# A scheduling edge that keeps the splits of a layer's q and k weights behind the exponentials written before them

## The chip, the cores and the metric

The kernel runs on one core of one Trainium2 chip. The metric is the device time of one launch in microseconds (us), taken as the median of several runs.

## The reference, cut to what matters

The program computes `x + attention(LN(x)) + stack(LN(x))` for 8 sequences of 512 tokens with 128 features. The attention has 16 heads of 8 features, relative positions and a causal mask. The stack has 6 layers, and nearly all of the time is spent in it. Each layer is a local attention (16 heads of 64 features, windows of 32 queries looking at 64 keys) and a gated feed-forward block:

```python
for i in range(DEPTH):                                   # DEPTH = 6
    x = attn_layer(shift_tokens(x), Wqkv[i], q_scale[i], k_scale[i], Wo[i]) + x
    x = ffn_layer(shift_tokens(x), ln_g[i], ln_b[i], W1[i], b1[i], W2[i], b2[i]) + x
# attn_layer: q, k, v = split(x @ Wqkv); q, k = l2norm(.) * scale, rotated by position
#   sim = q k^T * 8 in windows, masked; softmax; times v; @ Wo
# ffn_layer: layernorm, h = xn @ W1 + b1, a * gelu(gate) @ W2 + b2
```

Everything is float32, and the result must be that of float32.

## The kernel before

**Splits.** TensorE multiplies in a rounded form of float32 (the type F32R in the code). Where this is too coarse, an operand x is kept as two parts: hi, x rounded to that form, and lo = x - hi. A product is then three matmuls (`product`, lines 670 to 672). The function `split` makes the two parts: ScalarE copies x into hi (line 658), and another engine, VectorE if none is named, subtracts (line 659). For the projections of q and k, both the stream of x (`xs_hi`, `xs_lo`) and the weights (`wqk_hi`, `wqk_lo`) are split.

**Tiles.** The stack works through 192 tiles of 128 tokens: 6 layers, in each 8 sequences, in each 4 tiles. This text numbers the tiles of a layer 0 to 31, so tile 5 of layer 2 is its sixth. A tile has these steps: `project` (three matmuls into `qk_ps`; VectorE multiplies by the tables, lines 799 and 800, giving `q` and `rot`; ScalarE squares, line 801; GpSimd adds, lines 806 and 808), `normalise` (VectorE computes 1/norm in a chain of small steps, lines 821 and 75 to 86, the last of which gives `rn`; GpSimd multiplies q and k by it, line 826), `turn_q` and `turn_k` (transposes on TensorE, line 845; ScalarE copies, line 848), `scores` twice (masks by matmul, line 867; scores, line 879; VectorE takes maxima `mx`, line 888; ScalarE 8 exponentials `pr` with their sums, line 892; after the second time VectorE inverts the sums, line 904, GpSimd scales `pr`, line 905, and VectorE transposes it, line 907), `values` (line 921; the rows are then moved to `vw` by DMAs that SyncE's queue issues, line 923), `attend` and `add`. The feed-forward block of a finished sequence is laid between the steps of the next tiles, in pieces.

**Order.** TensorE's order is written out by hand: the strings `ORDERS` give the steps of a tile, with a period of four tiles, and the loop stands under `tc.manual_schedule(engines={nc.tensor.engine})`. On the other engines and in SyncE's DMA queue the order is chosen when the program is built: a planner runs through a timeline of its own and places an instruction where it finds it ready, which may be long before its place in the source. Each engine then runs its instructions strictly in that order, and waits in it. An edge added by `tc.add_manual_dep` with the class NoSync costs no semaphore; it only tells the planner that one instruction may not be placed before another.

Such edges exist already: `in_turn` chains the exponentials and the Gelus of the stack with each other, so that ScalarE's function tables are not exchanged more than needed. `last["any"]` holds the newest of them.

**The weights of the next layer.** While layer l is worked on, the weights of layer l+1 are fetched. The table `AHEAD` gives the place in the source:

```python
AHEAD |= {28 - 3 * c: ("projection", (c,)) for c in range(4)}
...
if n > -1 and left in AHEAD and l + 1 < DEPTH:
    step, args = AHEAD[left]
    fetch_of[step](l + 1, *args)
```

`left` is the number of tiles left in the layer. So in the source the four quarters c0 to c3 of `Wqk` are loaded and split at the start of the tiles 4, 7, 10 and 13 of the layer before. `load_projection` moves a quarter by DMA into a buffer `wqk_raw` and splits it. These buffers carry the tag `raw`, of which there are two in all; the two halves of W1 of the feed-forward block (`load`, tile 5 in the source, DMA line 680), the four quarters, and the blocks `wv_raw` and `wo_raw` (DMA lines 737 and 739) share them. A DMA into a `raw` buffer waits in SyncE's queue until the buffer's last user is done, for a quarter its subtraction, and the moves to `vw` issued later stand behind it. The parts hi and lo themselves have places of their own that alternate by layer. The quarters of layer 0 are loaded before any exponential of the stack.

Of the kernel before, what the change touches and what calls it, by code (L numbers as in the profile page):

```python
# [624 lines left out]
def steps_of_layers(ctx, tc, i, ident, ident_b, xt, out, spare):  # L625
    nc = tc.nc
# [8 lines left out]
    last = {}  # L635
# [17 lines left out]
            )  # L653
        last["any"] = ins

    def split(hi, lo, x, lo_engine=None):

        nc.scalar.copy(hi, x)
        (lo_engine or nc.vector).tensor_sub(lo, x, hi.bitcast(F32))  # L659

    def root_tile(n):
# [12 lines left out]
    def load(l):  # L674

        w = {}
        w["1"] = [p2.tile([P, 2 * DFF], F32R, name=f"w1_{k}", bufs=1) for k in ("hi", "lo")]
        for c in range(0, 2 * DFF, DFF):
            raw = wp.tile([P, DFF], F32, name="w1", tag="raw", bufs=2)
            nc.sync.dma_start(out=raw, in_=i["W1"][l, :, c : c + DFF])  # L680
            split(*(x[:, c : c + DFF] for x in w["1"]), raw)
        if VAR["D"]:
            raw = wp.tile([P, len(FCH), E], F32, name="w2", tag="raw", bufs=2)
        else:
            raw = w["2f"] = p2.tile([P, len(FCH), E], F32, name="w2", bufs=1)
        if VAR["D"]: w["2"] = [p2.tile([P, len(FCH), E], F32R, name=f"w2_{k}", bufs=1) for k in ("hi", "lo")]
        for n, (c, m) in enumerate(FCH):
            nc.sync.dma_start(out=raw[:m, n, :], in_=i["W2"][l, c : c + m, :])
        for n, (c, m) in enumerate(FCH if VAR["D"] else ()):
            split(*(x[:m, n] for x in w["2"]), raw[:m, n])  # L690

        w["g"] = p2.tile([P, 3], F32, name="wg")
        for n, k in enumerate(("ln_g", "ln_b", "b2")):
            nc.sync.dma_start(out=w["g"][:, n : n + 1], in_=i[k][l].unsqueeze(1))
        w["b1"] = p2.tile([P, 2, len(FCH)], F32, name="wb1")
        for a in range(2):
            for n, (c, m) in enumerate(FCH):
                nc.sync.dma_start(
                    out=w["b1"][:m, a, n : n + 1],
                    in_=i["b1"][l, a * DFF + c : a * DFF + c + m].unsqueeze(1),  # L700
                )
        return w
# [19 lines left out]
    def load_projection(l, c):  # L722

        raw = wp.tile([P, 512], F32, name="wqk_raw", tag="raw", bufs=2)
        nc.sync.dma_start(out=raw, in_=i["Wqk"][l, c])
        hi = by_turns[l % 2].tile([P, 512], F32R, name=f"wqk_hi{c}")
        lo = by_turns[l % 2].tile([P, 512], F32R, name=f"wqk_lo{c}")
        split(hi, lo, raw)
        projections.setdefault((l, c // 2), []).append((hi, lo))

    def load_values(l):
# [369 lines left out]
    for c in range(4):  # L1101
        load_projection(0, c)
        if c % 2:
            yield
# [40 lines left out]
    with tc.manual_schedule(engines={nc.tensor.engine}):  # L1145
        for n in range(-1, len(tiles) + 2):
# [11 lines left out]
            if n > -1 and left in AHEAD and l + 1 < DEPTH:  # L1158
                step, args = AHEAD[left]
# [127 lines left out]
```

## Time and profile before

| what | value |
|---|---|
| median of 3 runs | 3420.91 us (3416.99 to 3425.21) |
| profiled execution | 3422.36 us, of it 3420.6 us in the profile's span |
| granted TensorE clock, mean | 0.992 |
| TensorE matmul / VectorE / ScalarE / GpSimd busy | 94% / 88% / 81% / 80% of the span |
| one layer of the stack, tile 0 to tile 0 | 478 to 488 us |

In the profile PE is TensorE, PEld its weight loads, DVE VectorE, ACT ScalarE, POOL GpSimd and SP SyncE; L and a number is a line of the kernel. The profile is of one execution; its own time is 1.45 us over the median of the runs. Idle time is put down to the event that ended it, by semaphores. The busy time of TensorE is modelled from pipelined starts. Times of day such as 1509.59 are microseconds from the span's start.

### The profile page before, as it was taken

Reading aid. Unit: us, or ns where it says so; the run is one execution under the profiler, and the core shown is the slowest. Engines: PE = TensorE matmul, PEld = TensorE weight load, DVE = VectorE, ACT = ScalarE, POOL = GpSimd, SP = SyncE. Lnnn points to the kernel's source line nnn. Section 1 sums busy time; section 2 is a strip of 40 time slices with the busy share of each in tenths; the row PEclk is TensorE's granted clock in tenths of the full one; section 3 lists DMA queues with packets and bytes.
Section 4 is the critical chain, followed back from the end, with each engine's and each line's share of the span. In section 5 each row is a group of like instructions: output and inputs, shape, how many; then the busy total and the mean of one; then the engine's idle time right before and its main releaser. Section 6 shows DMA issues by size and latency. Waiting matters only on the chain.

```text
span 3420.6 us, 132912 instructions
## 1 busy us (share of the span) xinstructions
PE 3207.7 (94%) x51264; PEld 2394.4 (70%) x51264; DVE 2998.4 (88%) x7542; ACT 2783.2 (81%) x9786; POOL 2752.1 (80%) x2102
## 2 busy tenths in 40 slices
PE   7999979999999999999999999999999999999997
PEld 4667657777777777667777767777767777776775
DVE  7777788999999999899898998989999898998994
ACT  5777768888888888888888888888888888887884
POOL 6767668888888888788888888888888887887883
PEclk9999999999999999999999999999999999999998
DMA  2111123332333323333233332323333233332332
GB/s 59 37 40 46 48 72 74 75 73 72 89 82 78 74 71 79 84 87 75 69 75 78 83 87 69 77 70 86 82 80 76 69 78 77 81 80 75 83 75 58
DMA packets 221067, 250.07 MB, mean 73 GB/s; under 512 B 73238, under 2 KB 115604, under 8 KB 220436
## 3 DMA queue, kind: packets, MB, share of 16 engines
q1 hardware_dynamic: 220148, 241.18, 28.4%
q8 instruction: 407, 6.67, 0.9%
q14 instruction: 224, 1.84, 0.2%
q10 hardware_dynamic: 288, 0.39, 0.1%
HBM read 26.92 MB, written 4.19 MB: 9 GB/s over the span
## 4 chain that ended last, share of the span: by engine, by line
PE 43%; DVE 27%; ACT 18%; issue 4%; DMA 3%; POOL 3%; SPq 2%; ACTq 0%; POOLq 0%; DVEq 0%
ACT pr L892 8%; PE y_ps L941 8%; PE qkT_ps L845 6%; PE sc_ps L879 4%; DVE q L799 4%; DVE rot L800 4%; PE f_ps L1054 3%; PE v_ps L670 2%; PE v_ps L671 2%; PE v_ps L672 2%; ACT sq L801 2%; DVE pT L907 2%; DVE mx L888 2%; PE qk_ps L670 2%; ACT L892 2%
## 5 line engine op out<-in xcount | busy, mean ns | idle before, releaser
L892 ACT ACTIVATE pr<-sc_ps,mx 128x64 f32<-128x64 f32 x3072 | 923.4, 348 | 96.9 <-DVE mx L888 92.6
L806 POOL TENSOR_TENSOR q<-q,rot 128x1024 f32<-128x1024 f32 x380 | 924.8, 2434 | 91.8 <-DVE rot L800 62.9
L826 POOL TENSOR_TENSOR q<-q,rn 128x1024 f32<-128x1024 f32 x380 | 717.4, 1909 | 4.1 <-DVE rn L86 3.8
L892 ACT ACTIVATION_READ_ACCUMULATOR pr<-sc_ps,mx 128x1 f32 x3072 | 719.5, 241 | 0.0
L801 ACT ACTIVATE sq<-qk_ps 128x512 f32<-128x512 f32 x768 | 469.7, 633 | 262.1 <-DVE rot L800 157.6
L905 POOL TENSOR_TENSOR pr<-pr,sm 128x1024 f32<-128x1024 f32 x192 | 365.7, 1905 | 337.9 <-DVE rn L86 188.7
L799 DVE TENSOR_TENSOR q<-qk_ps,wrot 128x512 f32<-128x512 f32 x768 | 523.1, 681 | 48.1 <-PE qk_ps L672 43.3
L800 DVE TENSOR_TENSOR rot<-qk_ps,wrot 128x512 f32<-128x512 f32 x768 | 520.6, 678 | 0.0
L921 ACT COPY v<-v_ps 128x512 f32<-128x512 f32 x768 | 469.7, 660 | 48.8 <-PE v_ps L672 21.9
L845 PE MATMUL qkT_ps<-ident,q 128*128 128x128 f32 x3072 | 480.0, 282 | 24.8 <-POOL q L826 15.0
L845 PEld LDWEIGHTS qkT_ps<-ident,q 128*128 128x128 f32 x3072 | 340.3, 141 | 148.4 <-POOL q L826 58.0
L879 PEld LDWEIGHTS sc_ps<-kT,qT 64*32 64x32 f32 x24576 | 272.8, 105 | 183.2 <-issue 182.4
L941 PE MATMUL y_ps<-vw,pT 128*32 128x128 f32 x11904 | 382.0, 275 | 2.8 <-DMA vw<-v 2.8
L941 PEld LDWEIGHTS y_ps<-vw,pT 128*32 128x32 f32 x11904 | 327.6, 110 | 57.5 <-issue 28.5
L670 PE MATMUL qk_ps<-wqk_hi,xs_hi 128*128 128x512 f32 x768 | 347.1, 452 | 5.9 <-ACT sq L801 2.5
L670 PE MATMUL v_ps<-wvo_hi,xs_hi 128*128 128x512 f32 x768 | 338.8, 441 | 7.3 <-ACT ys L952 6.2
L879 PE MATMUL sc_ps<-kT,qT 64*32 64x64 f32 x24576 | 335.5, 225 | 0.0
L672 PE MATMUL qk_ps<-wqk_hi,xs_lo 128*128 128x512 f32 x768 | 304.5, 396 | 0.9 <-POOL xs_lo L659 0.9
L672 PE MATMUL v_ps<-wvo_hi,xs_lo 128*128 128x512 f32 x768 | 304.1, 396 | 0.0
L671 PE MATMUL qk_ps<-wqk_lo,xs_hi 128*128 128x512 f32 x768 | 303.7, 395 | 0.0
L671 PE MATMUL v_ps<-wvo_lo,xs_hi 128*128 128x512 f32 x768 | 302.7, 394 | 0.0
L888 DVE TENSOR_REDUCE mx<-sc_ps 128x4 f32<-128x256 f32 x768 | 282.4, 407 | 10.7 <-PE sc_ps L879 9.0
(206 smaller groups left out, 7058.9 us busy)
## 6 DMA issues: line engine op xcount, KB each, us to landing
vw<-v SPq DMA_DIRECT2D x3072, 64.0 KB
a_qz<-a_qT SPq DMA_DIRECT2D x128, 64.0 KB
wqk_raw<-in_Wqk SPq DMA_DIRECT2D x24, 256.0 KB
wv_raw<-in_WvT SPq DMA_DIRECT2D x12, 256.0 KB
wo_raw<-in_Wo SPq DMA_DIRECT2D x12, 256.0 KB
wrot<-in_trig SPq DMA_DIRECT2D x24, 128.0 KB
a_x<-in_x SPq DMA_DIRECT2D x8, 256.0 KB
a_res<-in_x SPq DMA_DIRECT2D x8, 256.0 KB
```

Source lines behind the costliest of these rows:

```text
L670: nc.tensor.matmul(ps, lhsT=ah, rhs=bh, start=True, stop=False)
L671: nc.tensor.matmul(ps, lhsT=ah, rhs=bl, start=False, stop=False)
L672: nc.tensor.matmul(ps, lhsT=al, rhs=bh, start=False, stop=True)
L799: nc.vector.tensor_mul(q[:, :, a], ps, wide(cos[:, a, :]))
L800: nc.vector.tensor_mul(v[:, :, 1 - a], ps, wide(sin[:, 1 - a, :]))
L801: nc.scalar.activation(sq[:, a], ps, AF.Square)
L806: adds.tensor_add(q, q, v)
L826: scales_by.tensor_mul(q, q, r[:, m, :].unsqueeze(2).to_broadcast([P, H, D]))
L845: nc.tensor.transpose(tr[:, m, :], q[:, 2 * hp : 2 * hp + 2, :].rearrange("p h d -> p (h d)"), ident)
L879: nc.tensor.matmul(ps[32 * j : 32 * j + 32, w, :], lhsT=qT[r, 4 * g + j, W * w : W * w + W], rhs=kT[r, 4 * g + j, W * w : W * w + 2 * W], ...
L892: nc.scalar.activation(pr[:, p, g, w, :], ps[:, w, :], AF.Exp, bias=mx[:, p, g, w : w + 1], accum_out=sm[:, m : m + 1],),
L941: nc.tensor.matmul(y[W * w : W * w + W, :], lhsT=pT[:, p, g, w, half, :], rhs=v[:, p, g, :], start=(p, g, half) == (0, 0, 0 if keys[w] is ...
```

## The change

`split` takes another argument, `after`. Where it is given, an edge without a semaphore keeps the ScalarE copy behind that instruction in the planned order. Only `load_projection` gives it: the newest exponential or Gelu at that place of the source. For layer 0 there is none yet. The subtraction has no edge of its own, but it reads the copy. The computation is unchanged.

```diff
-    def split(hi, lo, x, lo_engine=None):
+    def split(hi, lo, x, lo_engine=None, after=None):
 
-        nc.scalar.copy(hi, x)
+        step = nc.scalar.copy(hi, x)
+        if after is not None:
+            tc.add_manual_dep(
+                step.ins,
+                after.name,
+                mybir.DependencyInfo(mybir.DependencyClass.NoSync, mybir.DependencyReason.DATA),
+                reason="in its turn",
+            )
         (lo_engine or nc.vector).tensor_sub(lo, x, hi.bitcast(F32))
...
         lo = by_turns[l % 2].tile([P, 512], F32R, name=f"wqk_lo{c}")
-        split(hi, lo, raw)
+        split(hi, lo, raw, after=last.get("any"))
```

## The prediction, on record before the changed kernel ran

> **What bounds the kernel now.** I read the busy table and the chain of the page first.
>
> ```profile
> PE 3207.7 (94%) x51264; PEld 2394.4 (70%) x51264; DVE 2998.4 (88%) x7542; ACT 2783.2 (81%) x9786; POOL 2752.1 (80%) x2102
> PE 43%; DVE 27%; ACT 18%; issue 4%; DMA 3%; POOL 3%; SPq 2%; ACTq 0%; POOLq 0%; DVEq 0%
> ```
>
> TensorE carries the time, but more than half of the chain lies on others: it stands in its fixed order whenever VectorE's maxima or ScalarE's exponentials are late. Next I took the start of each tile's first mask matmul (line 867) from TensorE's timeline. Without weight work, four tiles of types 0, 1, 2, 3 (number modulo 4) take 13.9, 16.3, 13.1 and 16.2 us. The view by stretches, cut at such starts, shows what fills them (columns: length, then busy time of TensorE, its loads, VectorE, ScalarE, GpSimd):
>
> ```profile
> 1493.20:1507.90 14.70, 13.03 (x241) 9.92 (x241) 12.42 (x24) 12.61 (x40) 9.58 (x6) 1.00 0.34 90
> 1507.90:1528.30 20.40, 16.71 (x241) 11.20 (x241) 19.25 (x42) 16.05 (x61) 14.97 (x9) 1.00 0.40 100
> ...
> 1541.40:1557.60 16.20, 15.67 (x253) 11.81 (x253) 15.85 (x35) 13.60 (x50) 14.61 (x8) 1.00 0.29 72
> 1557.60:1571.50 13.90, 12.97 (x242) 9.93 (x242) 11.52 (x28) 13.30 (x47) 9.86 (x7) 1.00 0.28 69
> 1587.70:1600.80 13.10, 13.00 (x246) 10.38 (x246) 12.42 (x41) 11.23 (x46) 12.01 (x8) 1.00 0.39 95
> ...
> 2964.20:2982.20 18.00, 16.24 (x241) 11.33 (x240) 15.31 (x38) 14.76 (x59) 14.86 (x9) 1.00 0.29 71
> ```
>
> These are tiles 4, 5, 7, 8 and 10 of layer 2, then tile 5 of layer 5, which splits W1 but no q and k weights. Tile 5 of layer 2 is a burst: VectorE is busy for 19.25 us. Tile 7 has VectorE full, tile 10 TensorE and nearly VectorE, tile 8 leaves VectorE 2.4 us.
>
> The third view is the timeline of VectorE and GpSimd. The first three lines are subtractions in layer 0, the others in layer 2:
>
> ```profile
> 469.75 0.68 DVE L659 TENSOR_TENSOR wqk_lo<-wqk_raw,wqk_hi 128x512 fp32r<-128x512 f32 x1
> 471.01 2.19 DVE L659 TENSOR_TENSOR wqk_lo<-wqk_raw,wqk_hi 128x512 fp32r<-128x512 f32 x1
> 478.15 1.18 DVE L659 TENSOR_TENSOR wqk_lo<-wqk_raw,wqk_hi 128x512 fp32r<-128x512 f32 x1
> 1509.59 2.34 DVE L659 TENSOR_TENSOR wqk_lo<-wqk_raw,wqk_hi 128x512 fp32r<-128x512 f32 x1
> 1514.95 1.53 DVE L659 TENSOR_TENSOR wqk_lo<-wqk_raw,wqk_hi 128x512 fp32r<-128x512 f32 x1
> ```
>
> ```profile
> 1509.48 1.90 POOL L905 TENSOR_TENSOR pr<-pr,sm 128x1024 f32<-128x1024 f32 x1 [6.70 <-DVE root_ps L84]
> 1512.18 3.76 POOL L826 TENSOR_TENSOR q<-q,rn 128x1024 f32<-128x1024 f32 x2 [0.79 <-DVE rn L86]
> ```
>
> Alone a subtraction takes 0.68 us. Beside a GpSimd instruction it ends 0.55 us after that one: 1509.48 + 1.90 = 1511.38 against 1509.59 + 2.34 = 1511.93, and 1515.94 against 1516.48.
>
> **What moves.** TensorE's order stays. In the planned orders of the two programs, per layer 1 to 4: c0's copy goes from the end of the layer before (1430.0, just ahead of layer 2) to tile 4; c1 to c3 go from the burst in tiles 4 and 5 to the starts of tiles 7, 10 and 13. In layer 0, c0 moves from just before the stack, c1 to c3 from tile 0. No instruction is added. Each copy stands behind the previous tile's exponentials, ahead of `ys`; each subtraction inside or just behind the 1/norm chain.
>
> **What it saves.** c0's old place was free: tile 31 takes 18.24 us before layer 2 as before layer 5, where no c0 is. For c1 to c3, tiles 4 to 8 take 78.52, 78.22, 77.85 and 77.89 us in layers 1 to 4, mean 78.12, against 75.39 in layer 5: 2.73 us a layer, 10.9 in all. The three subtractions there took 0.70 + 2.34 + 1.53 = 4.57 us, so 0.60 of VectorE's time reached TensorE. In layer 0 the three took 0.68 + 2.19 + 1.18 = 4.05; at 0.60 that is 2.4 (bounds 0 and 4.05). Together 13.3 us.
>
> **What it costs.** I follow each subtraction at its new place in layer 2. The GpSimd instruction that runs at that moment:
>
> ```profile
> 1490.18 1.91 POOL L905 TENSOR_TENSOR pr<-pr,sm 128x1024 f32<-128x1024 f32 x1 [1.58 <-DVE root_ps L82]
> ...
> 1539.90 1.04 POOL L1002 TENSOR_TENSOR dg<-ident,rstd_lo 128x512 fp32r<-128x512 f32 x1
> ...
> 1585.67 1.91 POOL L905 TENSOR_TENSOR pr<-pr,sm 128x1024 f32<-128x1024 f32 x1 [0.84 <-DVE rn_s L81]
> ```
>
> - *c0, tile 4*, before line 84, which began at 1490.39. It ends at 1492.09 + 0.55 = 1492.64. The first `rot`, now two steps behind line 84, ends near 1494.15 instead of 1492.24. ScalarE's square waits for that `rot`, and Gelu, the exchange of tables and the exponentials stand behind it. TensorE's next scores waited 0.91 us for those exponentials: 1.9 us late. The planner also lets GpSimd's `xs_lo` and one addition pass ahead of the scaling of q: the transposes of q could then be 2.5 us late.
> - *c1, tile 7*, before line 82 (1540.32): it ends at 1540.94 + 0.55 = 1541.49. 1.2 us; VectorE then runs without a gap up to the maxima.
> - *c2, tile 10*, before line 85 (1586.29): it ends at 1588.13. 1.8 us on the maxima (1590.77), the exponentials (1591.37) and the second mask matmul, which follows their end with no gap.
> - *c3, tile 13*, behind line 86. Its copy, at `ys`'s place (1630.01 + 0.62), would free it at 1630.66; `pr`'s scaling starts at 1630.59 and lasts 1.91. If GpSimd is first, `q` moves from 1631.13 to 1633.05, and through ScalarE's squares, which free TensorE's buffers, about 1.8 us reach TensorE; if not, 0.2.
>
> The Trainium skill, page "SBUF — State Buffer", section "SBUF: two separate sides", says that whichever of two such instructions starts first holds the shared port for its whole length; by it those 0.07 us decide c3: the five layers together would pay 5 x 1.8 = 9 us as listed, and 5 x 0.2 = 1 us if the order turned round. No run here shows it for so close a start.
>
> The copies (0.62 us each) lie ahead of waits in which ScalarE stands anyway (0.75 to 1.44 us before the squares of tiles 7, 10 and 13; in tile 4 for the late `rot`) and are free; without that cover they would cost 20 x 0.62 = 12.4 us. DMAs: W1's second half now waits in SyncE's queue for c0's buffer (1492.64 instead of the layer's start), lands some 3 us later, and is split at 1501.6. c3, `wv_raw` and `wo_raw` wait in the queue for the subtractions in tiles 7, 10, 13, and `vw` moves behind them; ScalarE's `v` copies waited 15.8 us in all for `vw`, so this is hidden, or up to 1 us a layer.
>
> A layer costs 1.9 + 1.2 + 1.8 + 1.8 = 6.7 us if all of it reaches TensorE, 4.0 if only 0.60 does, as in the burst. Tiles 7 and 10 have no room, tile 8 some; I take the middle, 5.4. Layer 0 has the same new places: 5 x 5.4 = 27.0, less 13.3: 13.7 us longer. The profiled execution would go from 3422.36 to 3436.1; against the median, 1.45 lower, 3434.6.
>
> **Rivals.**
> - *A, the spread is free.* The splits fall into gaps, and only the burst goes: 3420.9 - 13.3 = 3407.6. For it speaks that VectorE leaves 2.4 us in tile 8 and that c0 cost nothing before. Against it, VectorE is 98% busy in tile 7. It decides from below 13.3 / 5 = 2.7 us a layer on. The skill's "Perfetto Trace Analysis", section "Optimization Strategy", says that interleaving stretches with different limits may help; it speaks for this case, and the sum by it would be this rival's. The rows of tiles 7 and 10 show the same engine short there.
> - *B, a draw.* GpSimd's instructions shift too, and the subtractions miss them: 20 x 0.68 = 13.6 against 13.3: 3421. Against it, `pr`'s scaling is released by line 904, just ahead of each subtraction.
> - *C, more than the sum.* Nothing is absorbed, and c0 costs 2.5: 5 x 7.3 = 36.5, with 1 us a layer for `vw` 41.5, less 13.3: up to 3449.
> - *That nothing moves* is out: all 20 copies stand elsewhere in the order.
>
> **The numbers.** Main case 0.68, A 0.10, B 0.13, C 0.09. The main case's own range is 5 x 4.0 less 15.0 to 6.7 x 5 less 10.9: 3426 to 3444. To hold 8 in 10 it reaches down to B and some way beyond, and part of the way to C: 3418 to 3446. Runs of this kernel tell about 0.2%, 6.8 us, from no change. Slower: 0.09 of C and nearly all of the main case, 0.72; within: B and the main case's edge, 0.18; faster: A, 0.10.
>
> **What would show it.** Right: tiles 4 + 5 of layers 1 to 4 only slightly shorter (34.8 to about 34), tiles 7, 10 and 13 longer by 1 to 2 us, subtractions of 1.2 to 2.4 us there. Wrong: subtractions of 0.7 us, or long ones with tiles 7, 10, 13 at 16.2, 13.1, 16.3 us; or tile 5 below 17 us.

## The result, and the profile after

| | median, us | runs | range, us |
|---|---|---|---|
| before, the same batch | 3421.75 | 5 | 3416.99 to 3425.21 |
| changed | 3434.46 | 5 | 3430.02 to 3440.38 |

The changed kernel is slower: the ratio is 1.0041, with a 95% interval of 1.0026 to 1.0056, or 12.7 us (9 to 19). The profiled execution took 3440.38 us (span 3438.7) at a granted clock of 0.990; it is the longest of the five, so its span difference of 18.1 us overstates the change by some 5 us. Lines from 667 on lie 8 higher in the listing than before: line 659 is still in `split` but now the copy, the subtraction is 667, the exponentials are 900, the scalings by GpSimd 834 and 913.

The busy table and the chain of the page hardly differ from before; VectorE's busy time is up by 11.4 us, and its share of the chain by one point:

```profile
PE 3215.0 (93%) x51264; PEld 2397.2 (70%) x51264; DVE 3009.8 (88%) x7542; ACT 2786.8 (81%) x9786; POOL 2756.3 (80%) x2102
...
PE 43%; DVE 28%; ACT 18%; POOL 4%; issue 4%; DMA 3%; SPq 2%; ACTq 0%; POOLq 0%; DVEq 0%
```

The place of the change shows in the stretches of layer 2, cut where TensorE begins a tile. These are tiles 4, 5, 7, 8 and 10 (columns: length, then busy time of TensorE, its loads, VectorE, ScalarE, GpSimd):

```profile
1499.60:1515.10 15.50, 13.21 (x242) 9.95 (x242) 14.09 (x29) 13.01 (x41) 9.67 (x5) 1.00 0.37 98
1515.10:1533.20 18.10, 16.16 (x240) 11.28 (x239) 15.39 (x38) 14.87 (x59) 14.84 (x9) 1.00 0.32 75
1546.30:1563.50 17.20, 15.69 (x253) 11.79 (x253) 16.55 (x39) 14.12 (x51) 15.39 (x9) 1.00 0.35 90
1563.50:1577.40 13.90, 12.84 (x242) 9.83 (x242) 11.40 (x29) 13.30 (x47) 9.61 (x6) 1.00 0.25 61
1593.90:1608.50 14.60, 13.34 (x247) 10.50 (x247) 13.85 (x45) 11.70 (x46) 12.43 (x8) 1.00 0.39 97
```

The burst is gone: tile 5 is down from 20.4 to 18.1 us and VectorE's busy time in it from 19.25 to 15.39. Tile 4 rose from 14.7 to 15.5, tile 7 from 16.2 to 17.2, tile 10 from 13.1 to 14.6. Tile 8, which has no split, is where it was.

The timeline of VectorE shows c0 to c3 of layer 2 at their new places, and that of GpSimd what each of them met:

```profile
1496.07 2.37 DVE L667 TENSOR_TENSOR wqk_lo<-wqk_raw,wqk_hi 128x512 fp32r<-128x512 f32 x1
1545.19 1.24 DVE L667 TENSOR_TENSOR wqk_lo<-wqk_raw,wqk_hi 128x512 fp32r<-128x512 f32 x1
1592.17 1.86 DVE L667 TENSOR_TENSOR wqk_lo<-wqk_raw,wqk_hi 128x512 fp32r<-128x512 f32 x1
1638.15 2.34 DVE L667 TENSOR_TENSOR wqk_lo<-wqk_raw,wqk_hi 128x512 fp32r<-128x512 f32 x1 [0.21 <-ACT wqk_hi L659]
```

```profile
1495.98 1.91 POOL L913 TENSOR_TENSOR pr<-pr,sm 128x1024 f32<-128x1024 f32 x1 [1.58 <-DVE root_ps L82]
1544.84 1.04 POOL L1010 TENSOR_TENSOR dg<-ident,rstd_lo 128x512 fp32r<-128x512 f32 x1
1591.58 1.90 POOL L913 TENSOR_TENSOR pr<-pr,sm 128x1024 f32<-128x1024 f32 x1 [0.85 <-DVE rn_s L81]
1638.04 1.90 POOL L913 TENSOR_TENSOR pr<-pr,sm 128x1024 f32<-128x1024 f32 x1 [3.85 <-DVE rn L86]
```

Each meets the GpSimd instruction that the prediction named, and ends 0.55 us after it: 1495.98 + 1.91 = 1497.89 against 1496.07 + 2.37 = 1498.44, and in the fourth pair 1639.94 against 1640.49. The four also show where in the stretches they lie: c2 runs from 1592.17, and the stretch of tile 10 begins at 1593.9. These subtractions, which the source puts at the start of a tile, start in the last 0.2 to 3.6 us of the stretch ahead of it, and their lateness is paid mostly in the stretch behind.

GpSimd is held as well. Where its next instruction begins before the subtraction has ended, that one takes longer too: the scaling of `pr` beside c1, before and after, is

```profile
1540.90 1.90 POOL L905 TENSOR_TENSOR pr<-pr,sm 128x1024 f32<-128x1024 f32 x1
```

```profile
1545.84 2.35 POOL L913 TENSOR_TENSOR pr<-pr,sm 128x1024 f32<-128x1024 f32 x1
```

So it is 0.45 us longer, at all five places of c1, and so is the first scaling of `q` behind all five of c3 (2.35 to 2.36 us instead of 1.90).

### The profile page after: what moved, and what is told of

It is laid out like the page before. It is cut to its first block, busy times and chain, and to the rows that moved or that the text cites. A ratio compares the mean times of both kernels' runs of the same rounds, so it can differ in the third digit from the quotient of the medians.

```text
span 3438.7 us, 132943 instructions
## 1 busy us (share of the span) xinstructions
PE 3215.0 (93%) x51264; PEld 2397.2 (70%) x51264; DVE 3009.8 (88%) x7542; ACT 2786.8 (81%) x9786; POOL 2756.3 (80%) x2102
## 4 chain that ended last, share of the span: by engine, by line
PE 43%; DVE 28%; ACT 18%; POOL 4%; issue 4%; DMA 3%; SPq 2%; ACTq 0%; POOLq 0%; DVEq 0%
ACT pr L900 8%; PE y_ps L949 8%; PE qkT_ps L853 6%; DVE q L807 4%; DVE rot L808 4%; PE sc_ps L887 4%; PE f_ps L1062 3%; PE v_ps L678 2%; PE v_ps L679 2%; DVE pT L915 2%; PE v_ps L680 2%; ACT sq L809 2%; ACT h L1040 2%; DVE mx L896 2%; ACT L900 2%
## 5 line engine op out<-in xcount | busy, mean ns | idle before, releaser
L929 ACT COPY v<-v_ps 128x512 f32<-128x512 f32 x768 | 471.9, 663 | 47.5 <-DMA vw<-v 17.3
L896 DVE TENSOR_REDUCE mx<-sc_ps 128x4 f32<-128x256 f32 x768 | 283.8, 410 | 11.7 <-PE sc_ps L887 10.1
```

## The experiments

Two batches were run, on two chips, beside that of the table above. Every time is compared with runs of the kernel before in its own batch: median 3420.28 us of 27 runs for the first four, 3423.55 us of 29 runs for the last four. Across batches only the ratios are compared.

All of them are read in one table: how much longer a tile is than in the kernel before, as the mean of layers 1 to 4 of one profiled execution, from the starts of the first mask matmuls (us). The first row is the length before. Over the four layers most entries agree within 0.35 us and all within 0.6 (tile 10 of the changed kernel: 1.40, 1.55, 1.46 and 1.35; its tile 4: 0.78 to 1.12).

| kernel | 3 | 4 | 5 | 7 | 8 | 9 | 10 | 11 | 12 | 13 | sum |
|---|---|---|---|---|---|---|---|---|---|---|---|
| before, length | 16.18 | 14.47 | 20.37 | 16.20 | 13.88 | 16.27 | 13.10 | 16.17 | 13.98 | 16.26 | |
| changed | +0.60 | +0.92 | -2.21 | +0.91 | 0.01 | +0.24 | +1.44 | -0.03 | -0.17 | +0.67 | +2.38 |
| e1_no_sub | +0.60 | -0.94 | -2.59 | -0.01 | 0.01 | +0.23 | -0.01 | +0.59 | -0.20 | 0.00 | -2.32 |
| e2_sub_gpsimd | +0.53 | -0.01 | -2.02 | +0.73 | -0.45 | +0.23 | 0.01 | +0.65 | +0.17 | 0.02 | -0.14 |
| e3_type0_start | 0.06 | -0.66 | -2.36 | +0.52 | +1.24 | 0.09 | 0.06 | +0.48 | +1.09 | 0.09 | +0.61 |
| e4_type0_late | 0.06 | -0.66 | -2.36 | -0.03 | +0.12 | +0.40 | 0.07 | -0.01 | 0.01 | +0.42 | -1.98 |
| e5_c0_free | 0.03 | -0.61 | -2.36 | +0.93 | 0.02 | +0.24 | +1.37 | 0.03 | -0.16 | +0.66 | +0.15 |
| e6_no_split | 0.00 | -0.57 | -2.36 | -0.03 | 0.01 | 0.01 | 0.10 | 0.02 | -0.03 | 0.00 | -2.85 |
| e7_late_c0_free | 0.01 | -0.59 | -2.37 | -0.15 | +0.10 | +0.40 | 0.00 | 0.02 | 0.01 | +0.42 | -2.15 |
| e8_late_gpsimd | 0.08 | -0.66 | -2.37 | -0.02 | +0.10 | +0.41 | 0.02 | -0.02 | 0.01 | +0.42 | -2.03 |

e3, e4 and e8 have two more places, in tiles 20 and 24, e7 one more, in tile 20; they are not in the sums and are given below.

**e1: the subtractions left out.** It is the changed kernel, but the 20 subtractions of layers 1 to 5 are not done and the high part stands for the low one as well, so part of the computation is missing.

```diff
-        (lo_engine or nc.vector).tensor_sub(lo, x, hi.bitcast(F32))
+        if lo is not None:
+            (lo_engine or nc.vector).tensor_sub(lo, x, hi.bitcast(F32))
...
-        lo = by_turns[l % 2].tile([P, 512], F32R, name=f"wqk_lo{c}")
-        split(hi, lo, raw, after=last.get("any"))
+        lo = hi
+        if "any" in last:
+            split(hi, None, raw, after=last["any"])
...
```

> The changed kernel without the 20 subtractions for the next layers' q and k weights; hi is used where lo would be, so a part of the computation is left out. The 20 ScalarE copies and all DMAs stay where the change put them. Theory (VectorE's subtractions at the new places are the whole cost): 20 subtractions cost 5.4 us a layer, 27 us in all, so 3434.5 - 27 = about 3407 us, with tiles 7, 10 and 13 back at 16.2, 13.1 and 16.3 us. Rival (the copies on ScalarE, held to the start of a tile ahead of ys, are the cost): no change, about 3434 us, tiles 7, 10 and 13 still longer by 0.7 to 1.5 us.

Measured: 3411.12 us, ratio 0.9973 (0.9964 to 0.9982), 0.0068 below the changed kernel: 23 us. Tiles 7, 10 and 13 are back at their old length, tile 4 is 1.86 us shorter than in the changed kernel. So the subtractions, with what they do to GpSimd beside them, make nearly the whole bill: in the sums of the table 4.7 of the 5.2 us by which the changed kernel stands above e6, which has no splits. But tiles 3 and 9, the ends of which hold the copies of c0 and c2, stay 0.60 and 0.23 us longer. Tile 3's is made up for behind it (tiles 4 and 5 come to -3.53 us here, against -2.93 in e6, which has no copies either), tile 9's is not. Tile 11 is 0.59 us longer here, and in e2, without being so in the changed kernel; no run explains that.

**e2: the subtraction on GpSimd.** The edge and the places in the source stay, but GpSimd subtracts. In its order the subtractions of c1 and c3 come a little later, in the stretches of tiles 7 and 13 themselves.

```diff
-        split(hi, lo, raw, after=last.get("any"))
+        split(hi, lo, raw, nc.gpsimd if "any" in last else None, after=last.get("any"))
```

> The changed kernel with the 20 subtractions on GpSimd instead of VectorE. Theory: VectorE's chain to the maxima is free again; GpSimd pays 1.1 to 1.2 us each (as its other 128x512 subtractions do). In tile 7 the scaling of q, which stands behind it, has no room (about 1.1 us), in tile 4, 10 and 13 it has some: 1 to 2.5 us a layer, so 3407 + 5 to 12 = 3412 to 3419 us. Rival (the copies are the cost): 3434 us. Rival (GpSimd at 75 to 92% busy in these tiles is as short as VectorE): 3430 us or more.

Measured: 3417.47 us, ratio 0.9994 (0.9985 to 1.0002), as expected, and not to be told from before. The summary of `wqk_lo` on GpSimd (least, median and most ns, then first and last start):

```profile
L667 POOL TENSOR_TENSOR wqk_lo<-wqk_raw,wqk_hi x20: 1268/1297/1312, 515.6 to 2603.1; 128x512 fp32r<-128x512 f32 x20
```

That is 1.30 us each time, more than VectorE's 0.68 alone, and yet tile 10 has none of its 1.44 us left and tile 13 none of its 0.67. So the work as such costs these tiles nothing where GpSimd does it. How much of the cost was VectorE's own 0.68 us and how much the holding of the two engines, e2 doesn't separate; but the 1.44 us of tile 10 are more than 0.68. In tile 7 GpSimd's own time is short: TensorE's transposes of q wait 1.32 us for its scaling there, and the tile keeps 0.73 us (0.45 of it comes back in tile 8). Of c0's cost in tiles 3 to 5 there stay 1.43 (-1.50 against -2.93 in e6); what keeps them was not tried.

**e3: roomy tiles, same place in the tile.** The prediction saw 2.4 us of VectorE's time free in tile 8. Here the splits stand in the source where tiles 8, 12, 20 and 24 start, all of the roomy type, with the edge as in the change.

```diff
-AHEAD |= {28 - 3 * c: ("projection", (c,)) for c in range(4)}
+AHEAD |= {(24, 20, 12, 8)[c]: ("projection", (c,)) for c in range(4)}
```

> The changed kernel with the four places moved to the starts of the tiles 8, 12, 20 and 24, where VectorE is busy for only 11.5 of 13.9 us. Rival (VectorE's room in a tile decides): the splits are free and the time falls by the whole cost, 3434.5 - 27 = 3408 us. Theory (the place in the chain decides: the subtraction waits for GpSimd's scaling of pr, and first rot, square, Gelu and exponentials stand behind it, as in tile 4): about 2 us each, 8 us a layer against 5.4: 3434.5 + 13 = about 3447 us.

Measured: 3444.00 us, ratio 1.0067 (1.0054 to 1.0079): the worst of all. Tiles 8, 12, 20 and 24 are longer by 1.24, 1.09, 1.19 and 1.19 us, and the tiles ahead of them (7, 11, 19, 23), in which the copies lie, by 0.48 to 0.54. VectorE and GpSimd at the first of the four places in layer 2, then the stretches of tiles 7 and 8:

```profile
1554.65 2.37 DVE L667 TENSOR_TENSOR wqk_lo<-wqk_raw,wqk_hi 128x512 fp32r<-128x512 f32 x1
```

```profile
1554.56 1.91 POOL L913 TENSOR_TENSOR pr<-pr,sm 128x1024 f32<-128x1024 f32 x1 [1.58 <-DVE root_ps L82]
```

```profile
1541.20:1557.90 16.70, 15.78 (x252) 11.76 (x251) 16.45 (x32) 13.18 (x49) 15.12 (x8) 1.00 0.27 66
1557.90:1573.20 15.30, 12.99 (x241) 9.83 (x240) 13.10 (x32) 14.08 (x48) 9.96 (x7) 1.00 0.34 88
```

The free time of tile 8 is not reached. The subtraction lies in the end of tile 7's stretch, in which VectorE is busy for 16.45 of 16.70 us, and it stands in the 1/norm chain just behind the line that lets GpSimd scale `pr`. Line 84, the next of that chain, begins only when it ends, at 1556.93. Tile 8 then still leaves VectorE 2.2 us, and is late all the same.

**e4: the same tiles, later in the tile.** The source places the split after the first eight exponentials of the tile, and a second edge without a semaphore keeps the subtraction behind the second pair of maxima. GpSimd is idle there.

```diff
-    def split(hi, lo, x, lo_engine=None, after=None):
+    def split(hi, lo, x, lo_engine=None, after=None, behind=None):
...
+        if behind is not None:
+            tc.add_manual_dep(
+                step.ins,
+                behind.name,
...
                 elif kind == "s" and have(n):
+                    first_half = last.get("any")
                     scores(n, k)
+                    if k == 1 and late:
+                        load_projection(*late, first_half)
```

> The same tiles 8, 12, 20 and 24, but the copy follows the first eight exponentials of the tile and the subtraction VectorE's second pair of maxima, where GpSimd stands idle for about 4 us before it scales pr and VectorE waits for TensorE later. Theory: subtractions of 0.68 us that reach TensorE hardly at all; the copy delays the square ahead of VectorE's sums by up to 0.5 us: 0 to 0.5 us each, 3407 to 3418 us. Rival (VectorE's room in the tile decides, not the place): the same time as the run with the splits at the start of these tiles.

Measured: 3413.33 us, ratio 0.9982 (0.9971 to 0.9992): faster than both the kernel before and the changed one. VectorE and GpSimd at the same subtraction:

```profile
1559.64 0.68 DVE L667 TENSOR_TENSOR wqk_lo<-wqk_raw,wqk_hi 128x512 fp32r<-128x512 f32 x1
```

```profile
1555.38 2.40 POOL L821 TENSOR_TENSOR q<-q,rot 128x1024 f32<-128x1024 f32 x1
1562.33 1.91 POOL L922 TENSOR_TENSOR pr<-pr,sm 128x1024 f32<-128x1024 f32 x1 [4.55 <-DVE root_ps L84]
```

GpSimd's work ends at 1557.78 and starts again at 1562.33; the subtraction lies between, in the stretch of tile 8 itself (1548.2 to 1562.3), and takes 0.68 us. All 20 do, against 2.36 at e3's places. A place now costs 0.01 to 0.17 us in its own tile and 0.40 to 0.42 in the next (tiles 9, 13, 21 and 25), together 0.52 on average instead of e3's 1.7. GpSimd is spared as well: in e3 its instruction behind each subtraction (`xs_lo`) took 1.54 to 1.75 us, in the kernel before at most 1.30. Place and meeting change together between e3 and e4, but the 1.7 us are more than the 0.68 of the work. The tiles don't account for all of the time gained: the tiles of the first five layers together are 1.0 us shorter in the profiled execution, and the medians differ by 7.0 us (by the interval, 2.7 to 9.9). In that execution the stack also began 6.7 us earlier and layer 5, which has no splits, was 4.5 us shorter; the start lies between 460.7 and 468.3 us over the ten profiles, and no run shows what moves it. So the gain is measured, but the tiles explain only a part of it.

**e5: only c0 goes back.** The edge is left out for c0 alone.

```diff
-        split(hi, lo, raw, after=last.get("any"))
+        split(hi, lo, raw, after=last.get("any") if c else None)
```

> The changed kernel, but c0 has no edge: the planner puts its split back at the end of the layer before; c1 to c3 stay in tiles 7, 10 and 13. Theory (c0's old place was free, its new one costs): in the changed kernel's trace tile 3 was 0.60 us longer than before, tile 4 1.5 and tile 5 0.15 longer than in layer 5; 2.2 us a layer go, 3434.5 - 11 = about 3423 us. Rival (c0 was free at its old place only while the burst behind it hid it): its cost shows in tiles 31 and 0 instead, and the time stays near 3434 us.

Measured: 3424.39 us, ratio 1.0007 (0.9997 to 1.0017), 0.0034 below the change: 11.6 us. Tile 3 loses its 0.60, and tiles 4 and 5 together come to -2.97 instead of -1.29; tiles 7, 9, 10 and 13 stay as in the changed kernel. So c0's place cost 0.60 + 1.68 = 2.3 us a layer, and its old place was indeed free, but only on the mean of the layers. There too the subtraction can meet GpSimd, as before layer 3 in the kernel before:

```profile
1917.25 1.92 DVE L659 TENSOR_TENSOR wqk_lo<-wqk_raw,wqk_hi 128x512 fp32r<-128x512 f32 x1 [0.68 <-ACT wqk_hi L658]
```

Tile 31, in which it lies, has 18.0 to 18.3 us in any case, and the tile behind it tells the difference. In the kernel before, e5 and e7 together, tile 0 of the next layer is 14.32 to 14.74 us long behind the seven subtractions that were held (1.49 to 2.26 us), and 13.41 to 13.43 behind the five that were not, or hardly (0.69 to 0.74). Without any split (e6) it is 13.99 to 14.12. Why a short one makes it shorter than none, no run shows.

**e6: no split at all after layer 0.** No load, no copy and no subtraction; the layers 1 to 5 use layer 0's weights, so part of the computation is missing.

```diff
     def load_projection(l, c):
 
+        if l > 0:
+            projections.setdefault((l, c // 2), []).append(projections[0, c // 2][c % 2])
+            return
```

> The changed kernel without any load or split of q and k weights after layer 0; the later layers use layer 0's, so this part of the computation is left out. Beside the run without the subtractions (3411.1 us) it shows what the 20 copies and their DMAs cost. Prediction's step (the copies are free): 3411 us again, and tiles 3 and 9 keep their 0.60 and 0.23 us. Rival (the copy, ahead of ys, kT and the v copies that free TensorE's buffers, costs those 0.83 us a layer): 3411.1 - 4 = about 3407 us, tiles 3 and 9 back at 16.2 and 16.3 us.

Measured: 3407.89 us, ratio 0.9954 (0.9939 to 0.9969). By the medians the price of all the splitting in the kernel before is 15.7 us (11 to 21). Its tiles 4 and 5 of layers 1 to 4 are 2.93 us shorter, 11.7 in all, the other tiles of the table within 0.1; the prediction's 2.73 for the burst was close. The rest isn't seen in the tiles. Against e1, which keeps loads and copies, the ratio is 0.0019 lower, or 6.5 us (the intervals just meet), more than the 4 us that were expected. In the tiles of the table the difference of the two is 0.53 us a layer, the most of it in tiles 9 and 11, so they show only a part of it.

**e7: late places and c0 free.** As e4, but c0 goes back to its old place, and c1 to c3 take tiles 8, 12 and 20.

```diff
-AHEAD |= {28 - 3 * c: ("projection", (c,)) for c in range(4)}
+AHEAD |= {(28, 24, 20, 12)[c]: ("projection", (c,)) for c in range(4)}
...
+                if step == "projection" and args[0]:
+                    late = l + 1, *args
```

> The run with late places in the tiles 8, 12, 20 and 24 (3413.3 us), with c0 back at its old place without an edge and c1 to c3 late in the tiles 8, 12 and 20. A late place cost 0.55 us in that trace (about 0.13 in the tile and 0.41 in the next). Theory: one of four goes in each layer, 5 x 0.55 = 2.7 us: about 3410.5 us. Rival (c0 isn't free at its old place): 3413 us or more.

Measured: 3415.44 us, ratio 0.9979 (0.9969 to 0.9989). The medians can't tell it from e4's 0.9982. The tiles can: tiles 24 and 25, in which e4 pays 0.17 + 0.42, are at 0.04 and 0.01, and no other tile pays for c0. Per layer one place is saved, 0.54 us, as expected.

**e8: e4 with the subtraction on GpSimd.** It was to tell whether the 0.5 us a place that e4 still pays is VectorE's 0.68.

```diff
-        split(hi, lo, raw, after=exps, behind=last.get("mx") if exps else None)
+        split(hi, lo, raw, nc.gpsimd if exps else None, after=exps, behind=last.get("mx") if exps else None)
```

> The run with late places (3413.3 us), with the subtraction on GpSimd, which stands idle there for 4 us (1.3 us each). If the 0.68 us of VectorE ahead of the 1/norm chain are what a late place costs, all of 20 x 0.55 = 11 us goes: about 3402 to 3405 us. If it is the copy on ScalarE, which delays the square, VectorE's sums and the maxima by up to 0.5 us, nothing goes: 3412 to 3414 us.

Measured: 3418.61 us, ratio 0.9990 (0.9982 to 0.9998), above both expectations by its median. But they were reckoned from e4's 3413.3 us in the other batch, and e4's ratio would be 3417.4 us in this one; the two intervals overlap, so the medians show no gain. In the table its row is e4's within 0.05 us: tiles 9, 13, 21 and 25 are 0.41 to 0.42 us longer here as there. The 0.4 us is therefore not VectorE's 0.68: without them on VectorE it stays. What both kernels share at these places is the load and the copy. In e4 the copy stands between the exponentials and a square:

```profile
1555.20 0.65 ACT L659 CAST wqk_hi<-wqk_raw 128x512 fp32r<-128x512 f32 x1
1555.71 0.64 ACT L816 ACTIVATE sq<-qk_ps 128x512 f32<-128x512 f32 x1
```

All that follows on ScalarE begins 0.5 us later, GpSimd's scaling of `q` among what comes of it, and TensorE's transposes wait for that one more often. Their idle time (us, times) before, in e4 and in e8:

```profile
  POOL q L826: 15.0, 17
```

```profile
  POOL q L841: 22.3, 35
```

```profile
  POOL q L841: 21.4, 34
```

The 17 to 18 waits more are nearly one for each of the 20 places, about 0.4 us each. That the copy and not the load makes them was not tried by itself.

## Why the prediction was right, point by point

The forecast was +13.7 us, the measurement +12.7 (3434.46 us against 3434.6). The direction held, and so did the main mechanism: the subtractions meet GpSimd, are held, and TensorE pays for the lateness. The way on which it reached TensorE was as said for c0 and c2 and another for c1 and c3. That the sum came within 1 us is luck in part: terms that were off cancelled, and of the range from 4.0 to 6.7 us a layer the middle was taken for the rough reason that some tiles have room and some have none.

- **The subtractions meet GpSimd: right.** Predicted lengths for layer 2 were 2.25, 1.2, 1.85 and, if GpSimd was first for c3, 2.4 us; measured 2.37, 1.24, 1.86 and 2.34. Rival B, that they miss, is out: the shortest is 1.22 us in layers 1 to 4 (0.96 in layer 0). That the meeting costs, and not the work alone: tile 10's 1.44 us and e3's 1.7 are more than the 0.68 of the work, and in e4, in the same tiles without a meeting, 0.52 are left. Subtractions of 0.68 us at the very places of the change were not run.
- **c3, the close start: the order was right, its price was wrong.** GpSimd began 0.11 us before the subtraction (1638.04 against 1638.15), and the subtraction took 2.34 us. The rule of the Trainium skill that the prediction weighed ("SBUF — State Buffer", section "SBUF: two separate sides": whichever starts first holds the port for its whole length) agrees with that, down to a start 0.11 us apart. But tile 13 grew by 0.67 us, not 1.8. The step that failed is "through ScalarE's squares, which free TensorE's buffers, about 1.8 us reach TensorE". The squares were late as said: the first began 2.17 us after `rn` before (1632.53 - 1630.36) and 3.99 after (1641.80 - 1637.81). But TensorE waits for no square in tile 13. Its first wait there is one for GpSimd, in the transposes of q, which waited for nothing before:

```profile
1634.41 0.66 PE L845 MATMUL qkT_ps<-ident,q 128*128 128x128 f32 x4
1632.45 3.77 POOL L826 TENSOR_TENSOR q<-q,rn 128x1024 f32<-128x1024 f32 x2
```

```profile
1642.31 0.66 PE L853 MATMUL qkT_ps<-ident,q 128*128 128x128 f32 x4 [0.49 <-POOL q L834]
1639.90 4.22 POOL L834 TENSOR_TENSOR q<-q,rn 128x1024 f32<-128x1024 f32 x2
```

  The first pair is before, the second after. The two scalings of q take 0.45 us longer, since the first is held by the subtraction, and the transposes come 3.95 us after the tile's start instead of 3.48. Waits for ScalarE's copies follow (0.16 us for one into `qT`), and TensorE is 1.06 us late at the second masks (8.87 instead of 7.81 after the tile's start), and 0.4 of that has come back when the next tile begins. VectorE, which was late by the subtraction's whole length, also made up a part. Further down its order stands an addition that waited for TensorE before and waits for nothing after:

```profile
1637.68 0.74 DVE L1066 SCALAR_TENSOR_TENSOR xt<-f_ps,wg,xt 64x512 f32<-64x512 f32 x1 [0.88 <-PE f_ps L1054]
```

```profile
1645.80 0.73 DVE L1074 SCALAR_TENSOR_TENSOR xt<-f_ps,wg,xt 64x512 f32<-64x512 f32 x1
```

  The 0.88 us gap took up about half of VectorE's lateness: the next `q` came 8.87 us after `rn` before and 9.52 after, 0.65 later. Which of the two chains sets the 0.67 us of the tile, no run separates.
- **c0, c1, c2: sized about right.** c0 was put at 1.9 (to 2.5) and cost 2.2 (tile 3 +0.60, tiles 4 and 5 -1.29 against -2.93 without any split); c1 1.2 against 0.91; c2 1.8 against 1.44, so tile 10, which has no room, let 0.8 of it through. TensorE's waits of layer 2 tell the way. For c0 they are 1.42 us for the Gelu and 0.62 for the scaling of q in tile 4, both of which the prediction named. For c2 it is the exponentials, as said: 0.89 us in tile 10, where it waited for none before, and 0.37 for a square. For c1 it is not the maxima and exponentials, for which it waits 0.45 us in tile 7 as before (0.47), but the scaling of q: 1.05 us. That one began 2.35 us after the tile's start instead of 1.40, behind the longer scaling of `pr` and the late `rn`.
- **The copies, "free": not quite.** The prediction had them ahead of `ys`, but counted only ScalarE's wait before the squares; `ys` is late by them, and TensorE's projections wait for `ys`. Of TensorE's weight loads, those that waited for `ys` (total us, times), before, changed, in e1 with copies but no subtractions, and in e6 without copies:

```profile
  PEld qk_ps L670: 8.6, 34
```

```profile
  PEld qk_ps L678: 14.3, 43
```

```profile
  PEld qk_ps L679: 13.0, 40
```

```profile
  PEld qk_ps L678: 9.5, 37
```

  The loads' waits grew by 5.7 us in all, most of it in e1 too, which also stands near the changed kernel in tiles 3 and 9. Tile 9 pays 0.24 us a layer for it, which was in no term; tile 3's 0.60 is counted in c0's cost above, and e1 made it up in tiles 4 and 5. The cost is far below the 12.4 us that the prediction gave without cover.
- **The sum of a layer.** 2.2 + 0.91 + 1.44 + 0.67 + 0.24 = 5.5 us, where the middle of 4.0 and 6.7 was taken, 5.4. The factor of 0.60 that made the lower end is not what happened: c0, c1 and c2 paid 0.76 to 1.2 of their price, c3 0.37 of it.
- **The savings.** The burst of layers 1 to 4: 2.73 a layer predicted, 2.93 by e6. Layer 0: 2.4 predicted for tiles 0 and 1, 1.27 in the changed kernel's trace (-0.35 and -0.92), 2.45 for tile 1 in e1. But e6, with no splits at all, is 1.43 longer in these two tiles (-0.44 and +1.87), so something else moves them too, and no run here prices this term. That c0's old place costs nothing the prediction read from tile 31; the tile that moves is 0, behind it, and it is only the mean over the layers that comes out near nothing (see e5).
- **The whole.** Layers 1 to 4: 4 x 2.49 us over tiles 3 to 13 and 19 to 25, and layer 0's tiles 2.33: 12.3 us against 12.7 measured. This leaves out 1.1 us a layer in tiles without a split of q and k weights, 0.61 of it in tile 30, which is 1.1 to 1.2 us longer in two of the four layers here and in two of them in e8 too. With them the tiles account for 16.7 of the 18.1 us of the profiled execution, the longest of the five. Rival A, that the spread is free, would have needed below 2.7 us a layer instead of 5.5.
- **The DMA queue: hidden, as said.** ScalarE's copies of `v` waited 15.8 us in all for `vw` before and 17.3 after.
- **Rival A's argument from room in a tile.** It counted VectorE's 2.4 free us in tile 8, but the splits of tile 8 run in tile 7's stretch, which has none: e3 paid 1.7 us a place, more than tiles 7, 10 and 13. The Trainium skill's advice to interleave stretches with different limits ("Perfetto Trace Analysis", section "Optimization Strategy") paid here only where the instruction really lies in the free time and clear of GpSimd, as in e4 and e7.

## What to carry to other kernels

A place in the source is not a place in time: read from the timeline what runs beside the moved instruction and who waits next, since the free time of the stretch that it is named after may lie behind it. Follow a lateness past its first waiter down to the next idle gap of the engine, and price a copy by what stands right behind it on its own engine. Here the edge alone loses 0.4%, and the same splits, moved to where GpSimd is idle (e4, e7), are about 0.2% faster than the kernel before and 0.6% faster than the changed one.

## What the runs showed of the hardware

One VectorE subtraction of 128x512 has lasted 0.68 us (e4, all 20) and 2.36 to 2.37 us (e3, all 20), by the GpSimd instruction beside it; in each pair shown above that met, it ends 0.55 us behind that instruction, however far that one had got. A start only 0.09 us (c0) or 0.11 us (c3) after GpSimd's was enough. It works the other way too: a GpSimd scaling that began while such a subtraction still ran took 2.35 to 2.36 us instead of 1.90 and ended 1.76 to 1.77 us after it (c1 and c3 of the changed kernel, all ten). The same subtraction on GpSimd took 1.27 to 1.32 us in every place tried (e2 and e8). For a VectorE step that would lie beside a GpSimd instruction of 1.9 us, the slower engine was the cheaper one here: the kernel's ratio is 0.9994 in e2 against 1.0041.
